# A graph network with all-adjacency layers: the next batch's adjacency loaded earlier, its sums regrouped over three stages, and the first batch reordered

## The chip, the cores and the metric

The kernel runs on one core of a Trainium2 chip. The core has five engines that each work through their own queue in order and wait for one another through semaphores: TensorE (PE in the profile) multiplies matrices into PSUM, VectorE (DVE), ScalarE (ACT) and GpSimd (POOL) work element by element, and SyncE (SP) starts the transfers between HBM and SBUF. The metric is the time of one execution on the device in microseconds, from the first to the last instruction.

## The reference, cut to what matters

Sixteen graphs with 1024 nodes of 128 features each. For each graph, a first network layer (here "first GNN") and then a network of four layers that all use the same 1024 x 1024 adjacency matrix. A layer needs the adjacency in both directions, once with its rows scaled to length one, once with its columns scaled to length one.

```python
def layernorm(x): return (x - mean(x)) / sqrt(var(x) + 1e-5)      # over the 128 features

degree = adj.sum(axis=-1)[:, :, None]                             # row sums
sum_neighbors = einsum('bid,bij->bjd', x, adj) / degree
x = layernorm(x + relu(concat([x, sum_neighbors]) @ W.T + b))

def l2norm(a, axis): return a / maximum(sqrt(sum(a * a, axis)), 1e-12)

def layer(nodes, adj, ws, bs, wd, bd, wn, bn, wu, bu):
    src_agg = einsum('bjv,bij->biv', nodes @ ws + bs, l2norm(adj, 2))   # rows scaled
    dst_agg = einsum('bjv,bji->biv', nodes @ wd + bd, l2norm(adj, 1))   # columns scaled
    return tanh(concat([src_agg, nodes @ wn + bn, dst_agg]) @ wu + bu)

# four layers; the third also takes the second's input, the fourth the input and the second's
x = layernorm(x + four_layers(x, adj))
```

So each adjacency needs three kinds of sums before it can be used: its row sums (degrees), the sums of squares of its rows, and the sums of squares of its columns.

## The kernel before, in words

**Tiling and stages.** One loop over the 16 batches `b`. In its four layers the loop works on batch `b`, whose adjacency `a` (natural layout, 1024 rows as 8 blocks of 128 on the partitions) and its transpose `at` lie scaled in SBUF. Between them it prepares batch `n = b + 1`: loading its adjacency `a2`, its sums, its scaling, its first GNN (between layers three and four) and its transpose. At the end of the loop body, `a2` becomes `a`. The adjacency has two buffers (pool `apool`).

**A layer** is `messages` and then `aggregate`. `messages` makes four groups of messages (`pt` in PSUM, L514; VectorE adds the bias, L517) and then, on VectorE, the sums and differences S3 (two halves, L529), S1 (L530), S2 (L531) and S4 (L532) of them. `aggregate` multiplies messages with quarters of the adjacency in the manner of a Strassen-Winograd scheme, seven products for eight: it needs combinations of the adjacency's quarters too (T for `a`, Q for `at`, made by `combine` on VectorE in layers one and four). Its loop issues steps of two matmuls (L692), each a pair of half-width columns, so a step works on the upper and lower half of the array at once. In a layer with n inputs, steps 0 to 2n - 1 are the node's own product, and then come the products. S3 is read first in layers one to three.

**The order** is written out by hand for TensorE, VectorE, ScalarE and GpSimd: each engine runs what the program issues, in that order. Two dictionaries put other work into it: `between` (a function after message group 0 to 3) and `hooks` (a function ahead of a given step). `events` inside `aggregate` put the reads of finished products at fixed steps in the same way. The order of transfers in SyncE's queue is the framework's own choice.

**Sums of the next adjacency** (`sums`, L237). For each of 8 row blocks: the degree (ScalarE with an accumulated copy for blocks 0 to 3, VectorE for 4 to 7), the squares with their row sum (ScalarE, L252, into a tile `sq` of which there are two buffers), and GpSimd's running sum of the squares over blocks, `acc` (L254 for the first, L256 for the others). `column_sums` (L259) transposes `acc` in squares of 32 and reduces it on VectorE into `part`; `inverses` (L288) multiplies `part` on TensorE (`pc`), picks the own groups on VectorE, and takes powers of -0.5 on GpSimd (L302). `inverse_rows` (L319) makes the inverses of columns and degrees and sends them to DRAM (`dr`), from where `factor_row` (L331) fetches them spread over all partitions as `cinv` and `dinv`. `scale_columns` (L338) multiplies the adjacency by `cinv` on VectorE, 16 times 128 x 512. `row_inverses` and `gather_inverses` (`sp` on VectorE, `rp` on TensorE, then `rinv`) make the factors of rows.

**Where they stood, in batches 1 to 14:** the load at step 5 of layer one; degrees and squares of blocks 0 to 7 at steps 1, 2, 4, 6, 12, 15, 18 and 20 of layer two; the column sums after message group 1 of layer three; the inverses at step 4, the factors at step 5 and the scaling at steps 12, 15, 19 and 25 of layer three.

**The norm of the previous batch** shares layer two: at step 0 `begin1` transposes the result (L349), adds the residual (L354) and reduces it to `s` (L356); at step 11 `centre1` multiplies `s` on TensorE (`pm`) and centres (L363); then squares, their sum and the power.

**The transpose.** Rows of the next adjacency are loaded a second time, in four parts of 256 rows (`load_rows`), scaled by `rinv` on ScalarE and transposed on VectorE (L473). Parts 2, 3 and, last, part 0 were put into the buffer of the current adjacency, blocks of which layer four no longer needs.

Of the kernel before, what the change touches and what calls it, by code (L numbers as in the profile page):

```python
# [8 lines left out]
F32 = mybir.dt.float32  # L9
AF = mybir.ActivationFunctionType  # L10
ALU = mybir.AluOpType
AX = mybir.AxisListType
# [11 lines left out]
def adj_resnorm_kernel(ctx: ExitStack, tc: tile.TileContext, x, adj, w0, b0, layers, out):  # L24
# [209 lines left out]
        for g in range(G):  # L234
            nc.sync.dma_start(ov[g, :, ks], ys[g * C:(g + 1) * C, ks])

    def sums(b, a, state, rows):  # L237

        if not state:
            state["cols"] = two.tile([P, 3 * NB], F32, tag="cols", name=f"cols{b}")  # L240
            state["acc"] = one.tile([P, N], F32, tag="row", name=f"acc{b}")
            state["inv"] = two.tile([P, C], F32, tag="inv", name=f"inv{b}")
            nc.gpsimd.memset(state["inv"][:, 3 * NB:], 0.0)
        cols, acc = state["cols"], state["acc"]
        for i in rows:
            sq = two.tile([P, N], F32, tag="sq", name=f"sq{b}_{i}")
            degree = cols[:, 2 * NB + i:2 * NB + i + 1]
            if i < BPH:
                nc.scalar.activation(sq, a[:, i, :], AF.Copy, accum_out=degree)
            else:  # L250
                nc.vector.reduce_sum(degree, a[:, i, :], axis=AX.X)
            nc.scalar.activation(sq, a[:, i, :], AF.Square, accum_out=cols[:, i:i + 1])  # L252
            if i == 1:
                nc.gpsimd.tensor_add(acc, state["sq"], sq)  # L254
            elif i > 1:
                nc.gpsimd.tensor_add(acc, acc, sq)  # L256
            state["sq"] = sq

    def column_sums(b, state):  # L259

# [27 lines left out]
    def inverses(b, state, first=0):  # L288

        cols = state["cols"]  # L290
        pc = small(f"pc{b}")
        by_halves(pc, fold, state["part"])
        own = one.tile([P, NH, G, BPH], F32, tag="own", name=f"own{b}")
        nc.vector.tensor_mul(own, pc.rearrange("p (h g k) -> p h g k", h=NH, g=G),
                             group[:, None, :, None].to_broadcast([P, NH, G, BPH]))
        nc.vector.reduce_sum(cols[:, NB:2 * NB].rearrange("p (h k) -> p h k", h=NH),
                             own.rearrange("p h g k -> p h k g"), axis=AX.X)
        root_inverses(cols, state["inv"], slice(first, 2 * NB))
# [549 lines left out]
    def to_x1(h):  # L848
        pt = product(f"x1tr_{h}")
        for q in range(BPH):  # L850
            nc.tensor.transpose(pt[:, q * P:(q + 1) * P], x1n[:, h * BPH + q], ident)
        nc.scalar.copy(x1T[:, half(h)], pt)
# [61 lines left out]
    for b in range(B):  # L914
# [6 lines left out]
        feats = [(x1T, 0)]  # L921
        f1 = feature(b, "f1T")
        if b == 0:
            def first_half0():
                nonlocal rinv
                to_x1(0)
                rinv = gather_inverses(0, row_inverses(0, inv))
                column_sums(0, st0)
                for q in (2, 3):
                    scale_rows(rows[q], q, rinv)  # L930

            t = messages(b, 0, feats, wm, {0: first_half0}, with_sums=False)
            cinv = {}

            def columns0(rows, h, engine=nc.vector):
                scale_columns(a, cinv[0], rows, half(h), engine)

            def rows0(destination, finish):
                for q in (2, 3):
                    transpose_rows(rows[q], q, at)  # L940

            def cinv0(destination, finish):
                cinv[0] = factor_rows_now(0, 1, inv, "cinv")

            def second0(destination, finish):
                columns0(range(NJ, NB), 1)
                destination(1, cinv[0])
                columns0(range(NJ), 1)

            def fold_and_scale(l, q):  # L950
                fold_begin(l, fetched[l])
                scale_rows(rows[q], q, rinv)

            def first0(destination, finish):
                columns0(range(NJ, NB), 0, nc.gpsimd)
                columns0(range(2), 0, nc.gpsimd)
                for q in (0, 1):
                    transpose_rows(rows[q], q, at)
                destination(0, cinv[0])
                columns0(range(2, NJ), 0)  # L960

            def sums0(destination, finish):
                combine_1(y)
                finish(1)
                combine(2, y, T)
                combine_1(yt)
                combine(3, y, T)

            def folded(l, part):
                return lambda *_: part(l, fetched[l])  # L970

            hooks = {2: lambda *_: inverses(0, st0, NB), 3: rows0, 5: folded(2, fold_begin), 7: cinv0,
                     8: folded(2, fold_end), 9: lambda *_: fold_and_scale(3, 0), 11: second0, 12: folded(3, fold_end),
                     14: lambda *_: scale_rows(rows[1], 1, rinv), 18: first0, 26: sums0}
            T = combined(0, "T")
            plain_layer(b, 0, feats, t, a, at, f1, "acc", hooks)
            wm = message_weights(b, 1)
            a2 = load(n)
            xs2 = load_spread(n)
        else:  # L980
            t = messages(b, 0, feats, wm)
            wm = message_weights(b, 1)
            w = {}
            Q = combined(b, "Q")

            def rows3():
                for q in (1, 0):
                    transpose_rows(rows[q], q, at)

            def next_rows(w=w):  # L990
                combine_1(yt)
                if nxt:
                    w["a"] = load(n)

            hooks = {0: rows3, 3: lambda: combine(4, y, T), 5: next_rows, 7: lambda: combine(2, yt, Q),
                     9: lambda: combine(3, yt, Q), 11: lambda: combine(4, yt, Q)}
            aggregate(b, 0, feats, t, a, at, T, Q, f1, "row", hooks)
            a2, xs2 = w.get("a"), None

# [3 lines left out]
        t = messages(b, 1, feats, wm)  # L1003
        wm = message_weights(b, 2)

        def sums_of(i):
            return lambda: sums(n, a2, st, (i,))

        hooks = {}
        if b == 0:  # L1010
            def quarters2():
                for i in (2, 3, 4):
                    combine(i, yt, Q)

            hooks = {0: quarters2, 12: lambda: combine(4, y, T)}
            hooks |= {5 + 2 * i if i < 3 else 4 + 3 * i: sums_of(i) for i in ALL}
        else:
            nm = f"1_{b - 1}"
            w = {"ys": summed(f"y{nm}", "xa")}
            sums_of_next = dict(zip((1, 2, 4, 6, 12, 15, 18, 20), map(sums_of, ALL))) if nxt else {}  # L1020

            def begin1(w=w, nm=nm):
                norm_spread(w["ys"], f4, KS)
                w["s"] = norm_sum(w["ys"], KS, nm, back)

            def centre1(w=w, nm=nm):
                w["sq"] = norm_centre(w["ys"], w["s"], KS, nm)
                if nxt:
                    w["xs"] = load_spread(n)

            def squares1(w=w, nm=nm):
                w["v"] = norm_squares(w["sq"], KS, nm)

            def rstd1(w=w, nm=nm):
                w["r"] = norm_rstd(w["v"], KS, nm)

            hooks = {0: begin1, 11: centre1, 14: squares1, 17: rstd1, **sums_of_next}
        aggregate(b, 1, feats, t, a, at, T, Q, f23, "acc", hooks)
        second_norm = w if b else None
        if b:  # L1040
            xs2 = w.get("xs")


        feats = [(f1, 1), (f23, 0)]
        w = {}

        def end1(w=second_norm):
            if b:
                norm_end(w["ys"], w["r"], KS)
                store(b - 1, w["ys"], KS)  # L1050

        def inverses3():
            inverses(n, st)
            end1()

        def start3(w=w):
            w["xT"] = to_features(xs2, f"x{n}_")
# [15 lines left out]
        def scale(i, h):  # L1073
            scale_columns(a2, w["cinv"], range(i, i + NJ), half(h))

        hooks, between = {4: end1}, {}
        if nxt:
            between = {1: sums3}
            hooks = {4: inverses3, 5: factors, 10: factors_of_rows, 11: start3, 12: lambda: scale(0, 1),
                     15: lambda: scale(NJ, 1), 18: factors_gathered, 19: lambda: scale(0, 0), 25: lambda: scale(NJ, 0)}  # L1080
        t = messages(b, 2, feats, wm, between)
        wm = message_weights(b, 3)
        aggregate(b, 2, feats, t, a, at, T, Q, f23, "acc", hooks)
# [9 lines left out]
        if nxt:  # L1093
# [42 lines left out]
                w["kept"] = put_aside(n, w["ys"])  # L1136

            def quarters0(w=w):
                w["T"] = combined(n, "T")
                for i in (2, 3):  # L1140
                    combine(i, y2, w["T"])
                scale_rows(rows[2], 2, rinv)

            def rows1(w=w):
                at2[1] = transposed(n, 1)
                transpose_rows(rows[2], 2, at2)
                scale_rows(rows[3], 3, rinv)
                w["back"] = take_back(b, kept)
                rows[0] = load_rows(n, 0, [place(0)])

            def rows2():
                transpose_rows(rows[3], 3, at2)
# [82 lines left out]
```

## Time and profile before

| | |
|---|---|
| time, median of 3 runs | 2473.33 us (2473.07 to 2473.34) |
| span of the profiled execution | 2472.0 us |
| TensorE busy | 2457.1 us, 99% of the span |
| VectorE, ScalarE, GpSimd busy | 1689.8, 843.1, 524.8 us |
| granted TensorE clock, mean | 0.998 |
| read from HBM, written | 199.17 MB, 18.46 MB: 88 GB/s over the span |
| chain that ended last | 97% TensorE |

Busy time is the union of an engine's instructions. Matmuls overlap in the array, so a busy TensorE says that matmuls are in flight, not that each runs at its best; whether it waits is seen from the starts of successive matmuls. An idle VectorE, ScalarE or GpSimd costs nothing as long as TensorE doesn't wait for it.

### The profile page before, as it was taken

To read this page: it belongs to the slowest core of one execution; us is meant where nothing else is said; L and a number is where in the kernel's file an instruction comes from. 1 tells how busy PE (TensorE), PEld (TensorE's weight loads), DVE (VectorE), ACT (ScalarE), POOL (GpSimd) and SP (SyncE) were. 2 spreads that over 40 slices of the span, in tenths; PEclk is the share of its full clock that TensorE was granted. 3 is DMA by queue.
4 is the path that set the end of the run, shared out by engine and by line. 5 is a ranking of instruction groups with operands and counts; after the bars stand their busy time and mean duration, and the time that the engine had idled before them with its cause. 6 is when DMAs were issued, how large, how long until landed. Compare 5 with 4: busy or idle time off the path is not lost.

```text
span 2472.0 us, 30281 instructions
## 1 busy us (share of the span) xinstructions
PE 2457.1 (99%) x11573; PEld 1037.2 (42%) x11573; DVE 1689.8 (68%) x2075; ACT 843.1 (34%) x1569; POOL 524.8 (21%) x205
## 2 busy tenths in 40 slices
PE   8999999999999999999999999999999999999998
PEld 5443344433444344443434444334443344433444
DVE  5858667586775857668577685776858667586743
ACT  5415234152341513425143341433415234152321
POOL 4401304013040220402104030040311304013000
PEclk9999999999999999999999999999999999999999
DMA  9517245261543516335172442724427244261410
GB/s 206 101 48 150 51 96 104 63 135 43 115 92 74 117 43 135 77 85 101 46 150 59 98 88 60 152 44 102 94 58 143 52 97 103 64 134 44 94 24 9
DMA packets 363793, 219.66 MB, mean 89 GB/s; under 512 B 150848, under 2 KB 334912, under 8 KB 363648
## 3 DMA queue, kind: packets, MB, share of 16 engines
q1 hardware_dynamic: 362880, 215.36, 41.3%
q0 software_dynamic: 768, 2.36, 0.4%
q8 instruction: 92, 1.51, 0.3%
q14 instruction: 53, 0.43, 0.1%
HBM read 199.17 MB, written 18.46 MB: 88 GB/s over the span
## 4 chain that ended last, share of the span: by engine, by line
PE 97%; DMA 1%; SPq 1%; DVE 0%; ACT 0%; issue 0%; POOLq 0%; DVEq 0%
PE m L692 44%; PE z L692 26%; PE pt L514 16%; PE pa L183 8%; PE pw L183 2%; DMA raw<-in_L_gnn_ws_dram 1%; SPq L458 0%; PE z L562 0%; PE pm L183 0%; DMA a<-in_adj_dram 0%; PE d L562 0%; DMA raw<-in_L_gnn_bs_dram 0%; DMA rows<-in_adj_dram 0%; DMA raw<-in_L_gnn_wn_dram 0%; SPq L131 0%
## 5 line engine op out<-in xcount | busy, mean ns | idle before, releaser
L692 PE MATMUL m<-Q,S 128*64 128x512 f32 x1008 | 446.4, 593 | 0.0
L692 PE MATMUL m<-T,S 128*64 128x512 f32 x1008 | 396.4, 593 | 0.0
L692 PE MATMUL m<-at,t 128*64 128x512 f32 x1008 | 393.5, 593 | 0.0
L692 PE MATMUL m<-a,t 128*64 128x512 f32 x1008 | 390.6, 593 | 0.0
L382 POOL TENSOR_TENSOR rs<-ve,mhalf 128x32 f32<-128x32 f32 x30 | 169.4, 5645 | 871.5 <-DVE ve L380 871.5
L517 DVE TENSOR_TENSOR t<-pt,wm 128x512 f32<-128x512 f32 x256 | 175.4, 690 | 188.6 <-PE pt L514 188.0
L692 PEld LDWEIGHTS m<-Q,S 128*64 128x64 f32 x1008 | 135.7, 137 | 270.8 <-issue 260.9
L256 POOL TENSOR_TENSOR acc<-acc,sq 128x1024 f32<-128x1024 f32 x90 | 220.1, 2446 | 82.2 <-ACT sq L252 79.8
L692 PE MATMUL z<-at,S 128*64 128x512 f32 x504 | 230.1, 594 | 0.0
L692 PE MATMUL z<-T,t 128*64 128x512 f32 x504 | 226.8, 592 | 0.0
L692 PE MATMUL z<-a,t 128*64 128x512 f32 x504 | 226.8, 592 | 0.0
L692 PE MATMUL z<-at,t 128*64 128x512 f32 x504 | 226.6, 592 | 0.0
L692 PE MATMUL z<-a,S 128*64 128x512 f32 x504 | 226.6, 592 | 0.0
L692 PE MATMUL z<-Q,t 128*64 128x512 f32 x504 | 226.6, 592 | 0.0
L596 ACT COPY e<-m 64x512 f32<-64x512 f32 x63 | 36.7, 582 | 528.0 <-PE m L692 527.7
L514 PE MATMUL pt<-wm,f1T 128*128 128x256 f32 x768 | 213.6, 383 | 0.1
L183 PE MATMUL pa<-a,xn 128*64 128x512 f32 x960 | 208.5, 592 | 0.0
L340 DVE TENSOR_TENSOR a<-a,cinv 128x512 f32<-128x512 f32 x250 | 156.7, 694 | 75.5 <-DMA cinv<-dr 73.0
L254 POOL TENSOR_TENSOR acc<-sq,sq 128x1024 f32<-128x1024 f32 x15 | 41.6, 2770 | 761.7 <-ACT sq L252 761.7
L692 PEld LDWEIGHTS m<-at,t 128*64 128x64 f32 x1008 | 120.2, 137 | 143.9 <-issue 143.9
L692 PEld LDWEIGHTS m<-T,S 128*64 128x64 f32 x1008 | 118.9, 137 | 135.4 <-issue 135.4
L692 PEld LDWEIGHTS m<-a,t 128*64 128x64 f32 x1008 | 119.0, 137 | 126.1 <-issue 117.3
(196 smaller groups left out, 3960.9 us busy)
## 6 DMA issues: line engine op xcount, KB each, us to landing
a<-in_adj_dram SPq DMA_DIRECT2D x120, 512.0 KB, 12.2
a<-in_adj_dram SPq DMA_DIRECT2D x360, 128.0 KB, 3.9
rows<-in_adj_dram SPq DMA_DIRECT2D x240, 64.0 KB, 2.9
wm<-wsave SPq DMA_DIRECT2D x16, 512.0 KB, 3.9
xn<-in_x_dram SPq DMA_DIRECT2D x124, 64.0 KB, 2.1
wm<-wsave SPq DMA_DIRECT2D x31, 256.0 KB, 2.7
xs<-in_x_dram SPq DMA_DIRECT2D x60, 128.0 KB, 3.6
cinv<-dr SPq DMA_DIRECT2D x30, 256.0 KB, 5.2
```

Source lines behind the costliest of these rows:

```text
L183: nc.tensor.matmul(out[s], x[:, s], y, start=start, stop=stop)
L254: nc.gpsimd.tensor_add(acc, state["sq"], sq)
L256: nc.gpsimd.tensor_add(acc, acc, sq)
L340: engine.tensor_mul(a[:, i, s], a[:, i, s], cinv[:, s])
L382: nc.gpsimd.tensor_tensor(rstd, ve, mhalf[:, :n], ALU.pow)
L514: nc.tensor.matmul(pt[:, q], f[:, i * P:(i + 1) * P], wm[:, 1 + c], start=(k == 0), stop=(k == nch - 1))
L517: nc.vector.tensor_add(t[j][:, o:o + 2].rearrange("p k a v c -> p k (a v c)"), pt, wm[:, 0][:, None, :].to_broadcast([P, 2, 2 * P]))
L596: nc.scalar.copy(e0[high], A[high])
L692: nc.tensor.matmul(o, x, y, start=start, stop=stop)
```

## The change

The change rearranges the preparation of the next adjacency in batches 1 to 14 so that less of it lies on VectorE and the scaling by columns is done sooner:

- `load(n)` ahead of layer one's messages, and the row sums of blocks 0 to 3 on ScalarE in layer one (steps 17 and 19); ScalarE also takes the row sums of blocks 4 to 7, in layer two. They are written over the block itself and no longer into `sq`.
- In layer two only squares are left for blocks 0 to 3: blocks 0 and 1 at step 1, then 2, 3, 4, ... at 3, 5, 8, 12, 15, 18. The column sums come at step 23, the inverses at step 29.
- In layer three the factors follow message group 0, the scaling is at steps 4, 6, 8 and 10, and the row factors at 12 and 17.
- To free the buffer for the early load, part 0 of the rows goes into two smaller tiles (`xa` and `acc`), and its load is asked for at step 18 of layer four and not 23.
- The power of the previous batch's norm comes after layer two, and its end at step 14 of layer three.
- In batch 0, the row factors and the column sums are put after message group 2 of layer one and not 0, the inverses at step 4 and not 2, the transposes of rows at 6 and not 3.

```diff
@@ sums of the next adjacency
+    def degree_of(a, state, i, engine=nc.scalar):
+        degree = state["cols"][:, 2 * NB + i:2 * NB + i + 1]
+        if engine is nc.vector:
+            nc.vector.reduce_sum(degree, a[:, i, :], axis=AX.X)
+        else:
+            nc.scalar.activation(a[:, i, :], a[:, i, :], AF.Copy, accum_out=degree)
+
+    def squares_of_row(b, a, state, i):
+
+        sq = two.tile([P, N], F32, tag="sq", name=f"sq{b}_{i}")
+        nc.scalar.activation(sq, a[:, i, :], AF.Square, accum_out=state["cols"][:, i:i + 1])
...
@@ batch 0, layer one
-            t = messages(b, 0, feats, wm, {0: first_half0}, with_sums=False)
+            t = messages(b, 0, feats, wm, {0: lambda: to_x1(0), 2: row_factors0}, with_sums=False)
...
-            hooks = {2: lambda *_: inverses(0, st0, NB), 3: rows0, 5: folded(2, fold_begin), 7: cinv0,
+            hooks = {4: lambda *_: inverses(0, st0, NB), 5: folded(2, fold_begin), 6: rows0, 7: cinv0,
@@ other batches, layer one
+            w = {}
+            if nxt:
+                w["a"] = load(n)
+                st = begin_sums(n)
             t = messages(b, 0, feats, wm)
...
-            def next_rows(w=w):
-                combine_1(yt)
+            def degrees(i, w=w, st=st):
                 if nxt:
-                    w["a"] = load(n)
-
-            hooks = {0: rows3, 3: lambda: combine(4, y, T), 5: next_rows, 7: lambda: combine(2, yt, Q),
-                     9: lambda: combine(3, yt, Q), 11: lambda: combine(4, yt, Q)}
+                    degree_of(w["a"], st, i)
+                    degree_of(w["a"], st, i + 1)
+
+            hooks = {0: rows3, 3: lambda: combine(4, y, T), 5: lambda: combine_1(yt), 7: lambda: combine(2, yt, Q),
+                     9: lambda: combine(3, yt, Q), 11: lambda: combine(4, yt, Q),
+                     17: lambda: degrees(0), 19: lambda: degrees(2)}
@@ layer two
-            sums_of_next = dict(zip((1, 2, 4, 6, 12, 15, 18, 20), map(sums_of, ALL))) if nxt else {}
+            sums_of_next = {}
+            if nxt:
+                sums_of_next = {1: sums_of(0, 1), 3: sums_of(2), 5: sums_of(3, of=(4,)), 8: sums_of(4, of=(5,)),
+                                12: sums_of(5, of=(6,)), 15: sums_of(6, of=(7,)), 18: sums_of(7),
+                                23: lambda: column_sums(n, st), 29: lambda: inverses(n, st)}
...
-            hooks = {0: begin1, 11: centre1, 14: squares1, 17: rstd1, **sums_of_next}
+            hooks = {0: begin1, 11: centre1, 14: squares1, **sums_of_next}
@@ layer three
-            hooks = {4: inverses3, 5: factors, 10: factors_of_rows, 11: start3, 12: lambda: scale(0, 1),
-                     15: lambda: scale(NJ, 1), 18: factors_gathered, 19: lambda: scale(0, 0), 25: lambda: scale(NJ, 0)}
+            scales = [lambda: scale(0, 1), lambda: scale(NJ, 1), lambda: scale(0, 0), lambda: scale(NJ, 0)]
+            if b == 0:
...
+            else:
+                between = {0: factors}
+                hooks = {**dict(zip((4, 6, 8, 10), scales)), 12: factors_of_rows, 14: end1, 17: factors_gathered, 20: start3}
@@ layer four
             def quarters0(w=w):
+                rows[0] = load_rows(n, 0, [one.tile([P, QB // 2, NH * P], F32, tag=tag, name=f"rows0_{n}_{tag}")
+                                           for tag in ("xa", "acc")])
...
-                rows[0] = load_rows(n, 0, [place(0)])
```

## The prediction

> **What bounds the kernel now.** I read four views in this order: the page (busy time by engine; first line below), TensorE's waits (next three lines: who waited for whom, us in total, times, longest), the matmul starts of one whole batch in the timeline, and then the timeline of VectorE (DVE), ScalarE (ACT) and GpSimd (POOL) at the places where the change moves work.
>
> ```profile
> PE 2457.1 (99%) x11573; PEld 1037.2 (42%) x11573; DVE 1689.8 (68%) x2075; ACT 843.1 (34%) x1569; POOL 524.8 (21%) x205
> ```
>
> ```profile
> PE w0tr L776 <- POOL ident masks.py:199: 4.4, 1, 4.4
> PE rp L183 <- DVE sp L307: 1.9, 1, 1.9
> PE pa L804 <- issue: 1.3, 1, 1.3
> ```
>
> TensorE is busy in all but 15 us, and its only large waits lie in the first 41 us. A batch takes 151.67 us: the chain has "PE pa L183 x64" at 603.12 and at 754.79. Inside a batch, matmul pairs start every 0.43 us with no hole. So nothing can gain more than the few us of the head, and anything that makes TensorE wait in a batch is paid 14 times (batches 1 to 14 have the changed path).
>
> A step of the aggregation loop is two such pairs, 0.857 us. For the batch that I follow, layer 2's messages begin at 538.21, its step 0 at 541.87 and its step 2 at 543.64. Here is what the other engines do there (start us, duration us, engine, line, operation, output and inputs, shapes, and in brackets the idle time before and who ended it):
>
> ```profile
> 539.06 0.72 ACT L705 ACTIVATE f1T<-e,bout 128x512 f32<-128x512 f32 x1 [1.21 <-DVE e L694]
> 539.68 1.04 ACT L249 ACTIVATE sq<-a 128x1024 f32<-128x1024 f32 x1
> ...
> 540.85 1.06 ACT L252 ACTIVATE sq<-a 128x1024 f32<-128x1024 f32 x1
> ...
> 543.07 1.06 ACT L252 ACTIVATE sq<-a 128x1024 f32<-128x1024 f32 x1
> ...
> 544.35 2.78 POOL L254 TENSOR_TENSOR acc<-sq,sq 128x1024 f32<-128x1024 f32 x1 [53.03 <-ACT sq L252]
> ...
> 542.70 0.76 DVE L529 TENSOR_TENSOR S<-t 128x256 f32<-128x256 f32 x2
> 543.50 0.69 DVE L530 TENSOR_TENSOR t<-t,t 128x512 f32<-128x512 f32 x1
> 544.22 0.69 DVE L531 TENSOR_TENSOR S<-t 128x512 f32<-128x512 f32 x1
> 544.95 2.73 DVE L532 TENSOR_TENSOR S<-t,S 128x512 f32<-128x512 f32 x1
> ...
> 550.13 1.22 DVE L356 TENSOR_REDUCE s<-y 128x32 f32<-128x1024 f32 x1
> ```
>
> The reader is to see L532: everywhere else it takes 0.69 us, here 2.73, ending 0.55 after GpSimd's add (544.35 + 2.78 = 547.13). L621 shows the same at 560.23 (2.31 for 0.69, under an add that ends at 561.99), while operations with a PSUM operand (L604) or one input (L251) keep their time under an add. And GpSimd's add takes 2.35 when it meets nothing, but 2.78 here, where it began inside L531: it ended 2.22 after L531 did.
>
> **What the Trainium skill says.** "SBUF — State Buffer", section "Who interferes with whom": a VectorE instruction with two SBUF inputs contends with a GpSimd instruction that reads SBUF; section "SBUF: two separate sides": it is an exclusive lock, whoever starts first holds it for the whole instruction and the other fully blocks. The trace agrees, with the numbers above. "TensorE: Matmul & The Clock Gate", Part 1: a long idle window (about 3.4 us) halves TensorE's clock until it has been busy again. The head agrees in kind: two 512-column matmul records take 1.92 us at 5.69 and 1.02 at 10.96; within the batches nothing shows it yet.
>
> **Head (batch 0).** The gather of the row inverses (rp) moves behind two more message groups, the column-sum matmul (pc) behind two more steps. The 1.87 us wait for sp goes: sp is ready at 40.0 and rp would now come near 41. Gain 1.8 us, once.
>
> **Loads and layer 1.** The load of the next adjacency goes ahead of layer 1's messages, because rows 0 no longer land in the current adjacency's buffer. The order of the DMA queue in the changed program shows a catch: the first of eight loads stands ahead of the second half of the rows-0 loads ("acc"), and waits for layer 4's last matmul (508.6) and transpose (508.74). Queued behind it: eight 64 KB loads, issued 0.5 us apart; a 512 KB load lands 5.2 us after issue (520.81 to 526.02), a 64 KB one in 2 to 3, and the eighth waits for the first load's landing. So rows 0 are complete at about 516.4. ScalarE scales four pieces (1.65 us) by 518.1; VectorE, busy until then, wants them at 519.1. Hidden. The other seven loads start near 514, land 2.5 us apart, and end near 534.4; the four row sums that ScalarE takes in layer 1 (4 x 1.1 us, from 525.9) need the first half, about 523.7, and end before its next read at 531.5. Hidden. Layer 2's weights, queued behind the load, land near 536, before 538.2. Hidden. Transposing rows 0 as four pieces (0.62 each) instead of two (1.17) adds 0.15 us to VectorE's chain, which reaches Q2 at 527.43 for a matmul at 527.81. Hidden.
>
> **Layer 2, first squares.** Before, ScalarE ran sum, square, sum, square, so the first add came at 544.35. With the sums gone it runs square, square from 539.68: the second starts at 540.74, and the add follows a square's start by 1.28: 542.02, ending 544.37. VectorE reaches its first two-input operation (L529, the first S3) only at 542.70: blocked, done at 544.65 (0.28 behind the add, for 256 elements). TensorE needs it at step 2, 543.64. Wait: 544.75 - 543.64 = **1.1 us**.
>
> **Layer 2, the lock again.** The next square may start when the add frees its buffer (544.40), so the second add comes at 545.63 to 545.68, and L531 (S2) would start at 545.75. The add comes first by a tenth and holds until about 548.06; S2 ends at 548.6; the third add (its square ready at 547.9) goes ahead of L532 and holds until 550.82; L532 ends at 551.37, not 547.68. Then the transpose (1.23), the addition L354 (two SBUF inputs, under the fourth add until 553.58, done 554.7) and the reduction L356 (1.22): 555.95. TensorE stands before pm at step 11: in the profile it starts at 551.40, just behind s (551.35), with no slack. With the first 1.1 it would come at 552.4. Wait: **3.6 us**. What stands behind pm in TensorE's queue is all the rest of the layer.
>
> **Layer 2, column sums.** They move from layer 3's messages to step 23, and their matmul to step 29, 18 steps after pm: 15.5 us. ScalarE's queue after pm: centre on VectorE 1.5, its square 1.1, sum and square 2.3, two m4 reads 1.2, sum and square 2.3, one read 0.6, last square 1.1 (the sums of rows 4 to 7 are new there, 1.1 each, moved from VectorE); then GpSimd's last add, held up by the sixth add and a VectorE operation, at pm + 13.6; the sum of the last two partial products (L613, two SBUF inputs, held to 0.55 behind that add), transpose 1.25, reduction 1.22: pm + 16.7. Wait **1.3 us** (1.0 to 1.4).
>
> **Layer 3.** From pc's vector step to the first scaling the profile has 579.21 to 592.12, 12.9 us (power on GpSimd 3.82, two DMA steps 7.6). Then 16 scalings (x 0.615 = 9.85) and sp: rp can start 23.3 us after pc. TensorE comes to rp (step 17) 23.2 after pc. Wait **0.2 us** (0 to 1). The messages are not held: VectorE's wait for the power ends before the fourth group's result is there.
>
> **Sum.** 2473.3 - 1.8 + 14 x (1.1 + 3.6 + 1.3 + 0.2 = 6.3, unrounded) = 2473.3 - 1.8 + 88.2 = **2559.7 us**. The work that VectorE loses (four sums of 1.21 a batch) brings nothing, since it isn't the bound.
>
> **Rivals.**
> 1. S2 wins the lock against the second add; the margin is a tenth. Then L532 follows the second add (549.2), L354 ends at 552.5, s at 553.8, the pm wait is 1.4 instead of 3.6: 14 x (1.1 + 1.4 + 1.4 + 0.2) = 57.4 less the head's 1.8: 2529.
> 2. The lock hardly hurts (VectorE gets in first): only pc and rp are left, 14 x 1.2 = 16.8: 2488. Against it: the add is 0.7 us ahead of L529.
> 3. Worse: the pm wait is as long as an idle window and now and then halves the clock, or rows 0 or the cinv row land 1 to 2 us later: above 2580.
> 4. No waits at all: the head's gain alone, 2471.5, no difference to be measured; against it, pm and rp have no slack.
> 5. Faster by over 0.2%: 5 us would have to come out of TensorE, and only about 4 us of idle time in the head is not start-up (1.3 + 1.9 and four waits of 0.2 to 0.3). Nothing in the profile for it.
>
> **How the numbers follow.** Forecast 0.42, rival 1 0.27, rival 2 0.14, rival 3 0.08, rival 4 0.06, rival 5 0.03. The range 2486 to 2580 holds the first three, 0.83, and takes in the ends of the unknown terms (pc 1.0 to 1.4, rp 0 to 1). Faster 0.03, same 0.06, slower the other 0.91.
>
> **What would show it.** In the changed profile: layer 2's first S3 subtraction (L529 before) lengthened to about 2 us under GpSimd's add; TensorE waits named S3, pm from s, pc from part, rp from sp, 14 times each; the period 157 to 158 us. Wrong would be: a period of 151.7; GpSimd's first add after S2; or waits in layer 1 (rows 0, late load) that I cost at nothing.

## The result, and the profile after

| | before | changed |
|---|---|---|
| time, median of 4 runs | 2473.23 us (2473.07 to 2473.34) | 2560.9 us (2558.78 to 2563.85) |
| ratio to before | | 1.0355 (95% interval 1.0337 to 1.0373) |
| span of the profiled execution | 2472.0 us | 2560.7 us |
| granted TensorE clock, mean | 0.998 | 0.988 |

The changed kernel is slower by 87.7 us; 2559.7 was predicted. The total is nearly the predicted one, but not for all the predicted reasons: one term that stood in the forecast hardly came, and one that was left out of it took its place. That the total fits is luck in this part.

The page of the changed kernel, busy time by engine (the last figure of each is the number of instructions):

```profile
PE 2498.3 (98%) x11573; PEld 1051.7 (41%) x11573; DVE 1687.6 (66%) x2049; ACT 890.4 (35%) x1681; POOL 509.5 (20%) x205
```

ScalarE took over sums (843.1 us before, 890.4 now). VectorE has 26 instructions fewer, yet its busy time fell by only 2 us: time blocked at the lock counts as busy. TensorE, with the same 11573 matmuls, is busy 41 us longer. A longer busy time for the same matmuls means that they ran further apart: a first hint, together with the mean clock, that the clock has a part in this.

TensorE's waits in the changed kernel (who waited for whom, us in total, times, longest):

```profile
PE pm L183 <- DVE s L358: 45.0, 14, 3.2
...
PE rp L183 <- DVE sp L309: 1.3, 3, 0.9
PE pc L183 <- DVE part L272: 1.2, 2, 0.6
```

The wait at pm has come, once in each of the 14 batches. The wait at pc came in two of them and not in fourteen; the one at rp in two and in the head. The wait for S3 is not in this list: the two halves of the array run out of step there, so one is always busy.

The timeline of the changed kernel in layer two of the batch that the prediction followed, ScalarE, GpSimd and VectorE (start us, duration us; step 2 would have begun at 552.0):

```profile
549.08 1.04 ACT L253 ACTIVATE sq<-a 128x1024 f32<-128x1024 f32 x1
...
552.74 1.06 ACT L253 ACTIVATE sq<-a 128x1024 f32<-128x1024 f32 x1 [2.53 <-POOL acc L256]
...
550.34 2.36 POOL L256 TENSOR_TENSOR acc<-sq,sq 128x1024 f32<-128x1024 f32 x1 [50.66 <-ACT sq L253]
553.96 7.90 POOL L258 TENSOR_TENSOR acc<-acc,sq 128x1024 f32<-128x1024 f32 x3 [1.26 <-ACT sq L253]
...
551.05 2.27 DVE L531 TENSOR_TENSOR S<-t 128x256 f32<-128x256 f32 x2
...
554.08 2.80 DVE L533 TENSOR_TENSOR S<-t 128x512 f32<-128x512 f32 x1
556.91 2.73 DVE L534 TENSOR_TENSOR S<-t,S 128x512 f32<-128x512 f32 x1
559.56 1.23 DVE L351 STREAM_TRANSPOSE y<-f23T 128x1024 f32<-128x1024 f32 x1
560.83 2.11 DVE L356 TENSOR_TENSOR y<-y,xk 128x1024 f32<-128x1024 f32 x1
562.98 1.22 DVE L358 TENSOR_REDUCE s<-y 128x32 f32<-128x1024 f32 x1
```

Read it as a relay for the lock. The first add holds it from 550.34 to 552.70 and blocks S3 (L531: 2.27 for its two halves, 0.76 before). Its end frees a square tile, ScalarE fills that from 552.74, and the second add comes at 553.96, 0.12 us ahead of S2 (L533: 2.80). The third add's square was done at 555.87, 1.0 us before S2 ended, and it goes next, ahead of S4 (L534: 2.73). The fourth goes ahead of the residual addition (L356: 2.11; 1.23 before). Four adds, and each time the VectorE operation waits for one of them. So s is ready at 564.20 instead of 551.35, in a timeline that lies only 8.35 us later.

TensorE's timeline of the same place (the bracket: idle before, and who ended it):

```profile
564.25 0.43 PE L183 MATMUL pm<-s,fold 128*64 128x32 f32 x4 [3.21 <-DVE s L358]
564.48 1.09 PE L694 MATMUL m<-T,S 128*64 128x512 f32 x1
...
565.37 1.06 PE L694 MATMUL m<-T,S 128*64 128x512 f32 x1
...
566.22 1.06 PE L694 MATMUL m<-T,S 128*64 128x512 f32 x1
```

After the wait, pairs start 0.85 us apart instead of 0.43, and last 1.06 instead of 0.59: half the clock. In this batch that goes on for seven pairs, some 2.7 us lost.

The record of the granted clock shows it as a step. Two windows around the wait (window, us, busy us and number for PE, PEld, DVE, ACT, POOL, granted clock, DMA share, GB/s):

```profile
559.69:563.10 3.41, 1.35 (x6) 0.18 (x2) 3.34 (x3) 1.45 (x3) 2.17 (x1) 1.00 0.00 0
563.10:566.51 3.41, 2.26 (x10) 0.98 (x12) 2.32 (x2) 0.47 (x1) 0.00 (x0) 0.50 0.91 127
```

The clock is halved from 563.10, while TensorE still waits, to 569.93. In each of these traces the changes of the clock lie on a grid of 3.413 us that runs through the whole execution, and a halved stretch inside it is one or two of these steps long. What decides is how much of a wait falls into one step. Over all the traces, the clock was halved at the end of every step in which TensorE had been idle for 2.06 us or more, never with 1.73 us or less, and both ways in between. So equal waits of 3.2 us can have unequal ends: the grid cuts the one shown 2.06 us after its start, and the clock falls; it cuts those of the first two batches at 1.96 and 2.01 us, and the clock stays.

Layer two as one window, before and then changed (columns as above):

```profile
538.20:568.10 29.90, 29.90 (x147) 11.66 (x145) 24.24 (x25) 20.10 (x34) 18.64 (x7) 1.00 0.30 58
```

```profile
546.80:583.00 36.20, 32.87 (x142) 12.66 (x143) 25.34 (x23) 19.34 (x34) 17.19 (x7) 0.91 0.20 40
```

The layer is 6.3 us longer: 3.3 without a matmul, the rest with matmuls that ran out of step (S3) or slowly (clock 0.91). Layer one, which took over the load and the row sums, lasts 29.80 against 29.54.

Setting each matmul's start beside that of the same matmul before gives the whole account, in us over the 14 batches: S3 16.2 (1.16 each), pm 46.7 (3.3 each), slow pairs between pm and the end of the layer 24.0 (in 12 batches, 1.3 to 2.8 each), pc 1.8 (0.9 in each of the two other batches), small shifts around pc 2.4 (about 0.2 a batch), all later stages together about 0. With the head, -2.2, that is 88.9, and the spans differ by 88.7. S3 and the slow pairs, 40.2, are about the time by which TensorE is busy longer (41.2).

### The profile page after: what moved, and what is told of

Its sections match the earlier page's. It is cut to its first block, busy times and chain, and to the rows that moved or that the text cites. A ratio compares the mean times of both kernels' runs of the same rounds, so it can differ in the third digit from the quotient of the medians.

```text
span 2560.7 us, 30532 instructions
## 1 busy us (share of the span) xinstructions
PE 2498.3 (98%) x11573; PEld 1051.7 (41%) x11573; DVE 1687.6 (66%) x2049; ACT 890.4 (35%) x1681; POOL 509.5 (20%) x205
## 3 DMA queue, kind: packets, MB, share of 16 engines
q0 software_dynamic: 768, 2.36, 0.4%
## 4 chain that ended last, share of the span: by engine, by line
PE 85%; DVE 10%; DMA 2%; ACT 1%; SPq 1%; issue 1%; POOL 0%; POOLq 0%; DVEq 0%; ACTq 0%
PE m L694 36%; PE z L694 23%; PE pt L516 15%; PE pa L183 8%; PE pw L183 2%; DVE S L533 2%; DVE S L534 1%; DVE S L531 1%; DVE y L356 1%; DVE a L342 1%; DVE s L358 1%; DVE y L351 1%; DMA a<-in_adj_dram 1%; DMA raw<-in_L_gnn_ws_dram 1%; DMA cinv<-dr 1%
## 5 line engine op out<-in xcount | busy, mean ns | idle before, releaser
L694 PE MATMUL m<-T,S 128*64 128x512 f32 x1008 | 420.1, 619 | 1.7
L694 PE MATMUL m<-at,t 128*64 128x512 f32 x1008 | 419.6, 618 | 0.0
L384 POOL TENSOR_TENSOR rs<-ve,mhalf 128x32 f32<-128x32 f32 x30 | 162.8, 5428 | 987.8 <-DVE ve L382 987.8
L258 POOL TENSOR_TENSOR acc<-acc,sq 128x1024 f32<-128x1024 f32 x90 | 229.3, 2547 | 151.6 <-ACT sq L253 148.3
L694 PEld LDWEIGHTS m<-T,S 128*64 128x64 f32 x1008 | 124.1, 142 | 177.0 <-issue 177.0
L256 POOL TENSOR_TENSOR acc<-sq,sq 128x1024 f32<-128x1024 f32 x15 | 35.7, 2379 | 728.9 <-ACT sq L253 728.9
```

What stands on the lines that cost most here:

```text
L256: nc.gpsimd.tensor_add(state["acc"], state["sq"], sq)
L258: nc.gpsimd.tensor_add(state["acc"], state["acc"], sq)
L384: nc.gpsimd.tensor_tensor(rstd, ve, mhalf[:, :n], ALU.pow)
L694: nc.tensor.matmul(o, x, y, start=start, stop=stop)
```

## The experiments

Two theories stood after the result. **A, the lock:** GpSimd's adds come before S3, S2, S4 and the residual addition, TensorE waits at S3 and pm, and the rest follows from that wait. **B, the regrouping:** the early column sums and inverses, the early load or ScalarE's longer queue cost the time. Eight kernels tell them apart. The kernel before measured 2472.95 us beside the first four and 2472.38 beside the last four. A label names each; where a kernel differs from the changed one, "changed" is the base.

**1. The head alone** (base: before).

```diff
-            t = messages(b, 0, feats, wm, {0: first_half0}, with_sums=False)
+            t = messages(b, 0, feats, wm, {0: lambda: to_x1(0), 2: row_factors0}, with_sums=False)
...
-            hooks = {2: lambda *_: inverses(0, st0, NB), 3: rows0, 5: folded(2, fold_begin), 7: cinv0,
+            hooks = {4: lambda *_: inverses(0, st0, NB), 5: folded(2, fold_begin), 6: rows0, 7: cinv0,
```

> The kernel before with only the reordering of batch 0. By the prediction: the 1.9 us wait of rp is gone and nothing else moves, 2473.2 - 1.8 = 2471.4 (the changed kernel's trace has TensorE 2.2 us ahead at the end of batch 0's first layer: 2471.0). If the reordering cost something later in batch 0, 2473 or more.

Measured: 2471.53 us, ratio 0.9996 (0.9988 to 1.0004). Its span is 2.3 us shorter than that of before, and the wait at rp went from 1.9 to 0.9, so only 1.0 of this comes from the wait itself; most of the rest is the clock (see the head in the account below). The gain is of the expected size, but too small for the times to prove.

**2. The column work back in layer three** (base: changed). Column sums, inverses, factors and scalings stand where they stood before; the early load, the sums on ScalarE and the squares' new places stay.

```diff
-                                12: sums_of(5, of=(6,)), 15: sums_of(6, of=(7,)), 18: sums_of(7),
-                                23: lambda: column_sums(n, st), 29: lambda: inverses(n, st)}
+                                12: sums_of(5, of=(6,)), 15: sums_of(6, of=(7,)), 18: sums_of(7)}
...
-                between = {0: factors}
-                hooks = {**dict(zip((4, 6, 8, 10), scales)), 12: factors_of_rows, 14: end1, 17: factors_gathered, 20: start3}
+            between = {1: sums3}
...
+            hooks = {4: inverses_and_end, 5: factors, 10: factors_of_rows, 11: start3, 18: factors_gathered,
+                     **dict(zip((12, 15, 19, 25), scales))}
```

> The changed kernel, but the column sums, their matmul, the inverses, factors and scalings stand in layer three where they stood before; the row sums in layer one and the squares of layer two stay as changed. Lock theory (GpSimd's adds, come 2.3 us earlier, block VectorE's two-input operations): the S3 wait (1.1), the pm wait (3.3) and the slow clock behind it (about 1.8) stay, only pc's 0.9 in some batches goes: 2555 to 2563. Rival (the column sums, the inverses and the scaling pulled forward are what costs): about 2472.

Measured: 2562.35 us, ratio 1.0359 (1.0344 to 1.0375), as slow as the changed kernel. TensorE's waits in it, in which pc doesn't appear:

```profile
PE pm L183 <- DVE s L358: 44.9, 14, 3.2
```

So in the kernel as it is, the early column sums and scalings cost nothing that shows in the time: the waits at pc went, but here all 14 batches had slow pairs after the same wait of 3.2 us, since the grid of the clock cut it elsewhere. What the early sums would cost without the wait at pm ahead of them, this run can't say; the fourth can.

**3. The early load alone** (base: changed). Row sums, squares, column sums and scalings stand at the steps of before; the load stays ahead of layer one, and row sums are still written over the block.

```diff
-                     17: lambda: degrees(0), 19: lambda: degrees(2)}
...
+                sums_of_next = {s: sums_of(i, of=(i,), engine=nc.scalar if i < BPH else nc.vector)
+                                for i, s in enumerate((1, 2, 4, 6, 12, 15, 18, 20))}
...
```

> The changed kernel with the early load, the two row tiles and batch 0's order, but row sums (VectorE again for blocks 4 to 7), squares, column sums and scaling where they stood before. Lock theory: ScalarE runs sum, square, sum, square again, the first add comes at the old place behind S2, no pm wait: 2471 to 2472. Rival (the early load and its transfers hold up layer one or two): 2480 or more.

Measured: 2495.82 us, ratio 1.0092 (1.0078 to 1.0106): a miss by 24 us. The timeline of this run, VectorE, ScalarE, GpSimd and TensorE:

```profile
546.27 2.73 DVE L534 TENSOR_TENSOR S<-t,S 128x512 f32<-128x512 f32 x1
...
550.19 2.98 DVE L356 TENSOR_TENSOR y<-y,xk 128x1024 f32<-128x1024 f32 x1
...
545.45 1.04 ACT L248 ACTIVATE a<-a 128x1024 f32<-128x1024 f32 x1
...
545.67 2.78 POOL L256 TENSOR_TENSOR acc<-sq,sq 128x1024 f32<-128x1024 f32 x1 [53.03 <-ACT sq L253]
549.71 5.66 POOL L258 TENSOR_TENSOR acc<-acc,sq 128x1024 f32<-128x1024 f32 x2 [1.26 <-ACT sq L253]
...
554.48 0.31 PE L183 MATMUL pm<-s,fold 128*64 128x32 f32 x4 [1.63 <-DVE s L358]
...
555.08 0.59 PE L694 MATMUL m<-T,S 128*64 128x512 f32 x1
...
555.50 0.59 PE L694 MATMUL m<-T,S 128*64 128x512 f32 x1
```

The same place before, ScalarE's third row sum, GpSimd's second add and the residual addition:

```profile
547.16 1.06 ACT L249 ACTIVATE sq<-a 128x1024 f32<-128x1024 f32 x1 [2.94 <-POOL acc L254]
...
549.64 5.12 POOL L256 TENSOR_TENSOR acc<-acc,sq 128x1024 f32<-128x1024 f32 x2 [2.51 <-ACT sq L252]
...
548.87 1.23 DVE L354 TENSOR_TENSOR y<-y,xk 128x1024 f32<-128x1024 f32 x1
```

S4 is blocked as it was before. New is the second add at 549.71, ahead of the residual addition (2.98 for 1.23), which makes s late by 1.6 us at pm, 14 times. I had overlooked why the second add comes sooner. Before, the third row sum was copied into the square tile that the first add still held, and waited for it (547.16); now it is copied over the block (545.45), so only the square waits, and the second add starts 4.04 us after the first and not 5.29. After this wait of 1.6 us, pairs start 0.42 apart at once: the clock stayed.

**4. The first add behind S4** (base: changed). A small GpSimd operation reads S4 and so holds the first add back until VectorE is past it.

```diff
-    def squares_of_row(b, a, state, i):
+    def squares_of_row(b, a, state, i, behind=None):
...
+            if behind is not None:
+                gate = one.tile([P, V], F32, tag="gate", name=f"gate{b}")
+                nc.gpsimd.tensor_add(gate, behind, behind)
             nc.gpsimd.tensor_add(state["acc"], state["sq"], sq)
...
-                    squares_of_row(n, a2, st, i)
+                    squares_of_row(n, a2, st, i, S[4][:, 0, 0] if b else None)
```

> The changed kernel with one more small GpSimd operation that reads S4 ahead of the first add of batches 1 to 14, so that the adds can't begin before VectorE has made all S. Lock theory: S3, S2 and S4 take 0.4 to 0.7 us again, s is ready near step 11, no slow clock; the wait of pc for part, which the slow clock had covered in most batches, comes back in all: 14 x 0.9 to 1.3, so 2471 + 13 to 18 = 2484 to 2489. Rival (ScalarE's longer queue or the early column sums hold TensorE up): stays near 2560.

Measured: 2536.52 us, ratio 1.0256 (1.0242 to 1.027): in the right direction, and a miss in size by about 50 us. Its waits, then VectorE and GpSimd in its timeline:

```profile
PE pc L183 <- DVE part L275: 43.6, 14, 3.1
```

```profile
552.22 0.69 DVE L537 TENSOR_TENSOR S<-t,S 128x512 f32<-128x512 f32 x1
...
554.10 2.59 DVE L359 TENSOR_TENSOR y<-y,xk 128x1024 f32<-128x1024 f32 x1
...
576.22 1.22 DVE L275 TENSOR_REDUCE part<-acct 128x32 f32<-128x1024 f32 x1
...
552.99 0.29 POOL L258 TENSOR_TENSOR gate<-S 128x64 f32<-128x64 f32 x1 [54.40 <-DVE S L537]
...
569.34 5.14 POOL L261 TENSOR_TENSOR acc<-acc,sq 128x1024 f32<-128x1024 f32 x2 [0.98 <-ACT sq L253]
```

S4 has its 0.69 back, and no wait at S3 or pm is left. But a TensorE that no longer waits there comes to pc too soon: the last add ends at 574.48 and part is ready at 577.44, so TensorE stands 3.1 us at pc, and the clock falls in 12 of the 14 batches. The mistake was to carry the 1.3 us of pc over from the prediction; it had been worked out with TensorE held at S3 and pm. Take that wait away, and the same column sums are too late by more.

**5. Both: column work late, first add behind S4** (2 and 4 together).

> The second experiment (column sums and scaling back in layer three) with the small GpSimd operation of the fourth: adds only after S4. The fourth had no pm wait and kept 3.1 us of pc; with pc back in layer three nothing is left: 2471 to 2472 by the theory that the lock and pc are the whole cost. If something else of the change costs (early load, row sums in layer one, ScalarE's longer queue): 2480 or more.

Measured: 2472.35 us, ratio 0.9999 (0.9991 to 1.0008). TensorE waits for nothing in a batch. The early load, the row sums in layer one and all eight sums on ScalarE are still in this kernel, and cost nothing that can be measured. What costs is the lock, and, once the lock no longer holds TensorE up, the early column sums.

**6. The early load, row sums into the square tile again** (base: 3).

```diff
-            nc.scalar.activation(a[:, i, :], a[:, i, :], AF.Copy, accum_out=degree)
+            nc.scalar.activation(into, a[:, i, :], AF.Copy, accum_out=degree)
...
+                    sq = square_tile(n, i)
+                    degree_of(a2, st, i, engine, sq)
```

> The third experiment, but the row sums' copies go into the squares' tile again, as before the change, and not over the block itself. In the third, ScalarE's copy of block 2 no longer had to wait for a free tile, so the second add came 1.25 us sooner, ahead of the addition of the residual (two SBUF inputs), which it blocked: 14 x 1.75 = 24.5 us of pm wait. If that is it: 2471 to 2472. If the early load causes it: 2495 again.

Measured: 2471.32 us, ratio 0.9994 (0.9986 to 1.0002). The second add stands 5.28 us after the first again (542.44 and 547.72), behind the residual addition (546.95, 1.23). So the 24.5 us of the third run came from the target of a copy that is made only for its sum. This is the lowest median measured, and its interval still includes 1.

**7 and 8. pm later, pm sooner** (base: changed). One number moves the place at which TensorE asks for s.

```diff
-            hooks = {0: begin1, 11: centre1, 14: squares1, **sums_of_next}
+            hooks = {0: begin1, 16: centre1, 19: squares1, **sums_of_next}
```

```diff
-            hooks = {0: begin1, 11: centre1, 14: squares1, **sums_of_next}
+            hooks = {0: begin1, 7: centre1, 14: squares1, **sums_of_next}
```

> The changed kernel with the centring (pm) at step 16 and the squares' sum at step 19 of layer two, not 11 and 14. The lock stays as it is; s is ready near the time of step 15. Theory: S3's 1.1 us stays, pm's wait and with it the slow clock go, pc at most 0.5: 2471 + 14 x 1.1 to 1.6 = 2486 to 2494, clock above 0.995. If the slow clock came from something else than the pm wait, it stays near 0.988 and the time 20 us higher.

Measured: 2488.16 us, ratio 1.0061 (1.0048 to 1.0075), clock 1.000, no wait at pm or pc. What is left over before is S3, which this edit doesn't touch (14 x 1.16 = 16.2), a little of rp, and the head's gain. The slow pairs went with the wait: two numbers give back 73 us, of which the pm waits are only 46.7.

> The changed kernel with the centring at step 7, four steps earlier. s is no sooner, so TensorE waits 3.4 us longer in each batch: 14 x 3.4 = 48 more than the changed kernel, and, if the slow clock follows from the length of the wait, it comes in every batch and longer (up to 1.7 us more each): 2609 to 2635. If the clock does not depend on the wait: 2609.

Measured: 2600.61 us, ratio 1.052 (1.0504 to 1.0536), clock 0.983: below what was expected. Its waits (the last of the 15 is 1.3 us, in the batch after the fourteen), and VectorE and ScalarE in its timeline:

```profile
PE pm L183 <- DVE s L358: 81.6, 15, 5.7
```

```profile
567.64 1.23 DVE L356 TENSOR_TENSOR y<-y,xk 128x1024 f32<-128x1024 f32 x1
...
571.97 1.06 ACT L368 ACTIVATE sq<-y 128x1024 f32<-128x1024 f32 x1 [9.17 <-DVE y L365]
```

Two things made it shorter. pm costs 6.14 us a batch, 2.8 more and not the 3.4 of four steps, because s came sooner: the norm's square now stands in ScalarE's queue ahead of the fifth square of the adjacency, whose add had met the residual addition, and waits for pm itself; so no add meets the residual addition (1.23). And all 14 batches show slow pairs after pm, but not more of them: what is left after S3 and pm is 25.3 us over the batches, about as much as in the changed kernel. The halved clock itself lasts longer: two steps of the grid in 11 batches of 14, where the changed kernel has two in 5 of 12, or 85 us against 58 in all. But 33 us of it fall into the waits, where nothing runs; behind them it is about the same, 53 us against 52.

## Why the prediction came out as it did

- **Head (batch 0):** near in size, -2.2 for -1.8, but the mechanism was only in part the forecast one. Of the 1.87 us wait at rp, 1.0 went. The larger part is the clock: in the profile of before it is halved just behind that wait, in the changed one it isn't. The window behind rp, before and then changed (columns as above):

```profile
40.96:44.37 3.41, 3.41 (x10) 2.70 (x9) 3.18 (x4) 3.41 (x10) 0.00 (x0) 0.50 1.20 239
```

```profile
40.86:44.27 3.41, 3.41 (x14) 2.07 (x15) 3.12 (x4) 2.93 (x8) 0.00 (x0) 1.00 1.20 220
```

  Eight message matmuls start 0.43 us apart there before and 0.21 when the clock is full, so 1.7 us; about 0.5 is lost again at another wait (bm, 0.2 before and 0.7 now). The forecast had none of the two, and that together they more than make up for the 0.9 us that stayed at rp is luck. Only one execution of before was traced, so how often its head loses this time isn't known.
- **Loads and layer 1:** right. No wait there, layer one is 0.3 us longer in its window, and run 5 keeps all of it at the time of before.
- **Layer 2, first squares:** right, 1.16 for 1.1. In the batch shown, the half of the array that reads S3 falls back by 1.15 us and the other by 0.34; so they run until pm, where the whole 1.16 counts.
- **Layer 2, the lock again:** right in mechanism and nearly in size, 3.3 to 3.4 for 3.6. The order that was forecast by a tenth of a microsecond held in every batch (0.11 to 0.12), and rival 1, where S2 wins, did not occur. The Trainium skill's "SBUF — State Buffer" ("SBUF: two separate sides") has the lock held for a whole instruction with the other fully blocked, and that is what each pair of lines above shows: S4 ended 0.55 us after the add that blocked it, so nearly all of its own 0.69 us was still to do.
- **Layer 2, column sums:** the mis-sized term. 1.3 us in 14 batches (18.2) was forecast; 0.9 came in two (1.8). The working was not far off for a TensorE at full clock, as those two show. In the other twelve, TensorE came to pc later, since its clock was halved on the way (by 1.3 to 2.8 us), and part was in time.
- **Layer 3:** forecast 0.2 in each batch, in fact nothing in most and 0.2 to 0.6 in a few, for the same reason where the layer before had been slow.
- **Left out of the forecast:** the slow clock after pm, 24.0 us. It stood only in rival 3, "now and then", with the time above 2580. It was not now and then but in 12 batches of 14, and yet the time stayed below 2580, since it paid for most of the 18.2 and 2.8 of pc and rp. So the sum is right within 1.2 us because errors of some 19 us and 24 us nearly cancel; only S3 and pm (63 us of 88) are right on their own. The forecast saw nothing of the clock in the batches of before, but the head had it, behind a wait of 1.9 us. The Trainium skill's "TensorE: Matmul & The Clock Gate" warns in "Why this matters for your kernels" of idle gaps of more than about 3 us between bursts, and says in Part 1 that the window of observation runs free. The grid of 3.413 us agrees with the second. On the first the measured bound is lower: what counts is the idle time inside one step of the grid, and about 2 us were enough. A wait of 3.6 us should have been priced with that.

What is shown: the lock and the early column sums carry the loss (runs 4 and 5), the slow clock goes with the wait at pm (run 7), and where the grid cuts a wait decides which batches are spared (the clock's record in the changed kernel and in runs 2, 4 and 8). What is not shown: why the clock goes both ways between 1.73 and 2.06 us of idle time. Nor did a run fill the wait with other matmuls, which would separate the halved clock from the wait.

## What to carry to other kernels

Taking work off an engine that isn't the bound can make the kernel slower, because what follows that work starts sooner and may meet something at a shared resource: before moving an operation, list what its end releases, and where that will be in the other engine's order. A wait behind another wait is not a constant: when the first one is taken away, the second must be worked out again with the engine arriving sooner. And a wait on TensorE can cost more than its length: those of 3.1 us and more mostly did here, by 1.3 to 2.8 us in the changed kernel, and the one of 1.9 us in the head did too. Here it was cheaper to ask for the result five steps later (run 7).

## What the runs showed of the hardware that was not expected

- Two engines at the lock alternate when both have an operation ready: in the changed kernel add, S3, add, S2, add, S4, add, residual addition. GpSimd's adds stand together in its queue, but a waiting VectorE operation gets in between each two. An add that waited for VectorE ends 2.2 us after VectorE's operation (a free one takes 2.36), and a waiting VectorE operation of 512 elements ends 0.55 after the add.
- The clock behaves as if judged step by step on a grid of 3.413 us that takes no notice of when a wait begins, and whose place differs from trace to trace. Waits of 1.6 us halved it in no batch of 14 (run 3), of 3.1 to 3.2 us in 38 of 42 (12, 14 and 12 of 14 in the changed kernel and runs 2 and 4), of 5.7 us in 14 of 14 (run 8). Once halved, it came back after a step with at most 0.60 us of idle time, and stayed halved for another step after 0.64 us or more. So where in a step a wait ends decides whether it costs one slow step or two.
- Where a copy that is made only for its sum puts its output can cost 24.5 us: its target tile is also what it waits for.
